# Layer 3 of a four-layer network summed before v is projected, its residual kept token-major, and the first layer's statistics on ScalarE

## The chip, the cores and the metric

The kernel runs on one core of one Trainium2 chip. The metric is the device time of the whole program in microseconds, the median of three runs. The engines are TensorE (PE, with PEld for its weight loads), VectorE (DVE), ScalarE (ACT), GpSimd (POOL) and SyncE (SP, which only issues transfers here).

## The reference

Sixteen images of 64 x 64 tokens with 256 channels in float32 go through four layers. Each layer adds to the residual what it makes of the group-normalised residual (32 groups):

```python
x = x + _L0_conv_ref(_gn(x), embeddings)      # nearest of 1024 code vectors, by distance
x = x + _L1_conv_ref(_gn(x), Wf, bf, ...)     # per row of 64 tokens: sigmoid(f g^T) h
x = x + _L2_conv_ref(_gn(x), w1, b1, ...)     # softmax over 4096 tokens of x0[i] x1[j]; a gate per token
x = x + _L3_conv_ref(_gn(x), w_qkv, w_out, b_out, gamma, beta)
...
def _L3_conv_ref(x, w_qkv, w_out, b_out, gamma, beta):      # 4 heads of 32
    q, k, v = jnp.split(jnp.einsum('bxyc,cf->bxyf', x, w_qkv), 3, axis=-1)
    q, k, v = (to_bhcn(q), to_bhcn(k), to_bhcn(v))
    q = jax.nn.softmax(q, axis=-2) * SCALE
    k = jax.nn.softmax(k, axis=-1)
    context = jnp.einsum('bhdn,bhen->bhde', k, v)
    out = jnp.einsum('bhde,bhdn->bhen', context, q)
    ...
    out = jnp.einsum('bxyh,hc->bxyc', out, w_out) + b_out
    mu = jnp.mean(out, axis=-1, keepdims=True)
    var = jnp.mean(jnp.square(out - mu), axis=-1, keepdims=True)
    return (out - mu) * jax.lax.rsqrt(var + LN_EPS) * gamma + beta
```

## The kernel before, in words

One image is one batch `b` of 4096 tokens, worked on in eight chunks of 512 tokens (four tiles of 128). The residual travels between layers through DRAM, channel-major: two blocks of 128 channels by 512 tokens, 512 KB a chunk. Each layer is a Python generator that emits its instructions and yields now and then. A heap of tasks with due times in units of a batch (`task`, the constants `LAG*` and `LEN*`) decides which generator emits next, so while one batch is in the search, the batches before it are in layer 1, in the exponentials of layer 2, in the gate and in layer 3. Blocks under `high_priority` are put ahead. A tile scheduler then lays the instructions into each engine's order and adds the waits; each engine works through its own order, and so does SP through its transfers.

The stages, with the lines of the profile:

- `stats0` (L298) takes the statistics of the input by DVE's `bn_stats` (L254). `gn_finish` turns statistics into scale and mean (L261 to L277).
- `stage1`, the search: `norm` (L327, L330) normalises on ACT; per tile of 128 tokens, PE makes the products with 1024 codes (`pd`, L382), ACT the norms (`nn`, L377), DVE finds the largest (L389, L394) and POOL gathers and adds the code to the tokens (L395). `back` transposes the chunk to channel-major (L357), ACT copies it out of PSUM (L360), DVE takes the next layer's statistics (L254, `st_s<-xt_s`), and ACT's queue stores it.
- `layer1`: projections (L465, L476), scores, tanh (L497), mixing (L509, L513).
- `rows2`, `stage2`: three rows of projections (L567), then 64 pairs a batch of an exponential over 2048 columns on ACT (`ex`, L619) and a product-and-sum on DVE (L622). `gate2` applies the gate (L675, L676) and takes statistics.
- `stage3`, layer 3, in two passes over the chunks. First pass: k (`pk`, L729) with a running maximum, exp (L738), q and v in one product of 256 columns a tile (`pqv`, L751), their bias as a row in three bfloat16 parts (`qv_row`, L755; `put_row` makes it), the transposed exp(k) (`ek`, L762, L764), q's softmax (maximum L770, subtraction on POOL L771, exp L772, sum L774, division on POOL L776), the context sum over k and v (`pc`, L780, L782), and one chunk later q transposed (L717, L719) and stored by ACT's queue. Between the passes the context goes through the output projection (`wctx`) and a Gram matrix (`gram`), from which the variance of an output row is q^T gram q. Second pass: `form` loads q and multiplies (`pz` L821, `qz` L823), `variance` sums by a product with ones (`pvr`, L829) and takes the power -1/2 on POOL (L832). The output is `po` (L849), scaled on ACT (L852), and the residual, read from DRAM again, is transposed with its row added (`pxo`, L854, L858) and added on DVE (L860).

The PSUM pool `ps_m` has four banks of 512 float32 columns, shared by all stages; `ps_w` has two of 1024.

Of the kernel before, what the change touches and what calls it, by code (L numbers as in the profile page):

```python
# [41 lines left out]
def kernel(  # L42
# [82 lines left out]
    def row_tile(name):  # L125
        t = const.tile([P, 2, C], BF16, name=name)
        nc.gpsimd.memset(t, 0.0)
        return t

    h_row, qv_row, x_row = row_tile("h_row"), row_tile("qv_row"), row_tile("x_row")  # L130

    def put_row(dst, v, weight, tag, plus=None):
# [4 lines left out]
        row = pb[:PARTS, :C]  # L137
        weight(row, v3, plus)

        for n in range(PARTS - 1):  # L140
            top = small.tile([PARTS, C], BF16, tag="ptop", name=f"top_{tag}_{n}", bufs=1)
            nc.scalar.copy(top, row)
            nc.tensor.matmul(row, lhsT=below[:, n, :], rhs=top, start=False, stop=True, skip_group_check=True)
        nc.scalar.copy(dst[0:PARTS, :, :], row.unsqueeze(1).to_broadcast([PARTS, 2, C]))
# [43 lines left out]
    w_src = w_qkv.rearrange("(k p) (s n) -> p k s n", p=P, s=3)  # L188


    gam = s3p.tile([P, C], F32, tag="v2", name="gam", bufs=5)
    nc.scalar.dma_start(out=gam, in_=gamma.rearrange("(o n) -> o n", o=1).to_broadcast([P, C]))

    def centred(src, name):
        t = const.tile([P, 2, C], F32, name=name)
        nc.scalar.dma_start(out=t[:, 0, :], in_=src)
        m = small.tile([P, 1], F32, tag="cen", name=f"cen_{name}")
        nc.vector.tensor_reduce(m, t[:, 0, :], AX.X, ALU.add)
        nc.vector.tensor_scalar(m, m, -1.0 / C, None, ALU.mult)
        nc.vector.tensor_scalar(t[:, 0, :], t[:, 0, :], m, None, ALU.add)  # L200
        nc.vector.tensor_tensor(t[:, 1, :], t[:, 0, :], gam, ALU.mult)
        return t

    wo2 = centred(w_out, "wo2")


    bo2 = centred(b_out.rearrange("(o n) -> o n", o=1).to_broadcast([P, C]), "bo2")
    nc.vector.tensor_scalar(bo2, bo2, float(DH ** 0.5 / HEADS), None, ALU.mult)

# [46 lines left out]
    def gn_finish(st, kind, b):  # L256

        tag = f"{kind}_{b}"
        mv = small.tile([P, NK, 2], F32, tag="gn_mv", name=f"mv_{tag}")
        for k in range(NK):  # L260
            nc.vector.bn_aggr(mv[:, k, :], st[:, k, :, :].rearrange("p c s -> p (c s)"))  # L261
        mean = mv[:, :, 0]
# [45 lines left out]
    def stage1(b):  # L308
        tag = f"s1_{b}"
        scale, _, nbias = norm0.pop(b)  # L310
# [39 lines left out]
        st1 = stats_tile(1, f"st1_{tag}")  # L350
        x1_d[b] = []

        def back(ch):
            for k in range(NK):
# [5 lines left out]
                nc.scalar.copy(xt[ch][:, k, :], pt)  # L360
            chunk_stats(st1, xt[ch], ch)
# [10 lines left out]
        for ch in range(NCHUNK):  # L372
            for t in range(CH):
# [27 lines left out]
                if t == 1:  # L401
                    if ch + 1 < NCHUNK:
                        norm(ch + 1)
                        yield 2
                if t == 2:
                    if ch + 1 < NCHUNK:
                        norm_rows(ch + 1)
                    if ch > 0:
                        back(ch - 1)
                        yield 2  # L410
                if t == 3:
                    if ch + 1 < NCHUNK:
# [4 lines left out]
        with tc.high_priority(offset=URGENT):  # L417
            norm1[b] = gn_finish(st1, "n1", b)
# [5 lines left out]
    def layer1(b):  # L424
# [34 lines left out]
        def attend(ch):  # L459
# [14 lines left out]
            for t in range(CH):  # L474
# [5 lines left out]
                if t % 2 == 1:  # L480
                    nc.tensor.matmul(
                        ph[:, t - 1 : t + 1, :], lhsT=ones3, rhs=h_row, start=False, stop=True, skip_group_check=True
# [207 lines left out]
    def stage3(b):  # L690
# [6 lines left out]
        wqv_n = wts.tile([P, NK, 2 * P], F32, tag="wqv_n", name=f"wqv_{tag}")  # L697
        nc.sync.dma_start(out=wqv_n[:, :, 0:P], in_=w_src[:, :, 0, :])
        nc.sync.dma_start(out=wqv_n[:, :, P:], in_=w_src[:, :, 2, :])
        with tc.high_priority(offset=URGENT):  # L700
            scaled(wk_n, scale, nc.scalar)
            scaled(wqv_n, scale, nc.vector)
            put_row(qv_row, nmean, by_weight(wqv_n), f"qv_{tag}")
# [6 lines left out]
        ctxa = wts.tile([P, P], F32, tag="ctxa", name=f"ctx_{tag}")  # L710
        qvs, qTs = {}, []
# [228 lines left out]
```

## Time and profile before

| | |
|---|---|
| median of three runs | 5996.47 us (5990.2 to 6000.28) |
| profiled execution: time, span | 5985.76 us, 5984.0 us |
| granted TensorE clock, mean | 0.949 |
| busy PE, DVE, ACT, POOL | 5310.6, 5132.9, 4756.8, 1873.7 us |
| DMA | 1059.10 MB, mean 177 GB/s |

A page of the profile lists each engine's busy time, the chain of work that ended last, and the costliest groups of instructions: line, engine, operation, output and inputs by the program's names, shape, count, busy time, mean duration of one in ns, then the idle time ahead of them and who ended it. A float32 product appears as two records on PE. A wait line gives the waiting engine and line, the one it waited for, the total in us, the number of times and the longest.

### The profile page before, as it was taken

What the parts mean: (1) busy time and instruction counts of PE and PEld (TensorE: products, weight loads), DVE (VectorE), ACT (ScalarE), POOL (GpSimd) and SP (SyncE); (2) the same over time, 40 slices, a digit from 0 to 9 for tenths busy, and PEclk for the clock granted to TensorE, in tenths of its full rate; (3) what the DMA queues carried; (4) which work ended last, traced back from release to release, by engine and by line L of the source; (5) the groups of instructions that cost most, each with busy time, mean ns of one, the idle gap of its engine ahead of it and who ended that gap; (6) DMA issues with size and microseconds to landing.
All of it is one profiled execution on the core that took longest, in us unless ns stands there. A gap on an engine that the chain in (4) does not pass through costs nothing.

```text
span 5984.0 us, 73947 instructions
## 1 busy us (share of the span) xinstructions
PE 5310.6 (89%) x25167; PEld 3208.0 (54%) x25167; DVE 5132.9 (86%) x7270; ACT 4756.8 (79%) x7138; POOL 1873.7 (31%) x1314
## 2 busy tenths in 40 slices
PE   8978798989989899998989989898999989887777
PEld 3535355545556465554646556464655646464445
DVE  6589698899989899898989989898998989888862
ACT  4578597878888797888979788797988879787763
POOL 3222224233332333323333332433333333312231
PEclk9989899999999999999999999999999999998788
DMA  6453645665656657565665746566475655545543
GB/s 185 143 160 112 209 132 186 187 187 158 207 165 201 194 160 227 149 210 163 197 212 156 224 151 207 172 199 203 153 223 160 204 183 172 188 140 176 170 144 111
DMA packets 521359, 1059.10 MB, mean 177 GB/s; under 512 B 52504, under 2 KB 266392, under 8 KB 512792
## 3 DMA queue, kind: packets, MB, share of 16 engines
q1 hardware_dynamic: 406288, 885.11, 44.6%
q0 software_dynamic: 73728, 67.14, 7.8%
q10 hardware_dynamic: 40968, 102.13, 4.5%
q8 instruction: 200, 3.28, 0.2%
q14 instruction: 175, 1.43, 0.1%
HBM read 751.18 MB, written 303.04 MB: 176 GB/s over the span
## 4 chain that ended last, share of the span: by engine, by line
PE 48%; DVE 21%; ACT 15%; issue 7%; DMA 5%; POOL 4%; ACTq 0%; SPq 0%; POOLq 0%; DVEq 0%
PE pd_s L382 16%; DVE ex_s L622 10%; ACT ex_s L619 6%; PE ph_l L476 4%; PE pqv_s L751 4%; PE po_s L849 3%; DVE i_s L394 2%; PE pk_s L729 2%; PE pr_r L567 2%; DVE nd_s L389 2%; PE po_l L509 2%; POOL xc_s L395 2%; PE pvr_s L829 1%; DVE st_s L254 1%; PE pc_s L780 1%
## 5 line engine op out<-in xcount | busy, mean ns | idle before, releaser
L622 DVE CUSTOM_DVE_ANT_0 ex_s<-ex_s,x2b 128x2048 f32<-128x2048 f32 x1024 | 2369.4, 2318 | 135.9 <-ACT ex_s L619 133.5
L619 ACT ACTIVATE ex_s<-x0b,nmax_s,x_r 128x2048 f32<-128x2048 f32 x1024 | 2138.8, 2089 | 64.7 <-DVE num_s L622 55.0
L382 PE MATMUL pd_s<-e,xn_s 128*128 128x512 f32 x4096 | 2013.5, 621 | 87.6 <-DVE m L389 63.8
L395 POOL DMA_INDIRECT xc_s<-in_emb_rows,i_s x512 | 1084.0, 2117 | 1962.9 <-DVE i_s L394 1460.6
L382 PEld LDWEIGHTS pd_s<-e,xn_s 128*128 128x128 f32 x4096 | 750.6, 196 | 830.4 <-issue 655.0
L389 DVE CUSTOM_DVE_ANT_0 nd_s<-pd_s,nn_s 128x1024 f32<-128x1024 f32 x512 | 620.5, 1212 | 114.8 <-PE pd_s L382 85.4
L394 DVE FIND_INDEX8 i_s<-m,nd_s 128x8 uint32<-128x1024 f32 x512 | 623.5, 1218 | 0.0
L377 ACT ACTIVATE nn_s<-ne,nx_s 128x1024 f32<-128x1024 f32 x512 | 585.1, 1145 | 10.6 <-DVE nx_s L348 3.4
L476 PE MATMUL ph_l<-wh_l,xt_l 128*128 128x256 f32 x2048 | 534.6, 396 | 28.6 <-DVE xt_l L513 20.6
L751 PE MATMUL pqv_s<-wqv_s,xk_s 128*128 128x256 f32 x2048 | 491.9, 381 | 2.9 <-ACT xt_s L360 2.9
L476 PEld LDWEIGHTS ph_l<-wh_l,xt_l 128*128 128x128 f32 x2048 | 381.7, 194 | 155.1 <-issue 61.2
L751 PEld LDWEIGHTS pqv_s<-wqv_s,xk_s 128*128 128x128 f32 x2048 | 388.4, 191 | 130.1 <-issue 63.3
L832 POOL TENSOR_TENSOR lrs_s<-lrs_s,mhalf 128x4 f32<-128x4 f32 x128 | 187.6, 1465 | 651.5 <-ACT lrs_s L831 638.0
L849 PE MATMUL po_s<-wctx_s,qo_s 128*128 128x256 f32 x1024 | 329.4, 412 | 63.5 <-ACT y_s L852 59.8
L852 ACT ACTIVATE y_s<-po_s,lrs_s 128x256 f32<-128x256 f32 x512 | 236.0, 470 | 147.5 <-PE po_s L849 104.3
L327 ACT ACTIVATE xn_s<-xt_s,nb_n,s_n 128x512 f32<-128x512 f32 x256 | 202.4, 806 | 108.2 <-DMA xt_s<-in_xT 98.6
L776 POOL TENSOR_TENSOR qv_s<-qv_s,qd_s 128x512 f32<-128x512 f32 x128 | 167.2, 1307 | 385.3 <-DVE qd_s L775 312.8
L509 PE MATMUL po_l<-attn,h_l 128*128 128x128 f32 x2048 | 280.7, 283 | 7.3 <-DVE m L389 5.2
L509 PEld LDWEIGHTS po_l<-attn,h_l 128*128 128x128 f32 x2048 | 259.9, 195 | 45.8 <-issue 22.1
L849 PEld LDWEIGHTS po_s<-wctx_s,qo_s 128*128 128x128 f32 x1024 | 178.0, 199 | 194.5 <-ACT y_s L852 123.9
L729 PE MATMUL pk_s<-xk_s,wk_s 128*128 128x512 f32 x512 | 256.6, 623 | 0.0
L860 DVE TENSOR_TENSOR y_s<-pxo_s,y_s 128x512 f32<-128x512 f32 x256 | 174.1, 683 | 91.4 <-ACT y_s L852 91.3
(197 smaller groups left out, 7707.6 us busy)
## 6 DMA issues: line engine op xcount, KB each, us to landing
xs_s<-in_xT SPq DMA_DIRECT2D x128, 512.0 KB
xt_s<-in_xT SPq DMA_DIRECT2D x128, 512.0 KB
xc_s<-in_x SPq DMA_DIRECT2D x128, 512.0 KB
x_s<-xt_s ACTq DMA_DIRECT2D x128, 512.0 KB
xt_l<-x_s SPq DMA_DIRECT2D x128, 512.0 KB
x_l<-xt_l SPq DMA_DIRECT2D x128, 512.0 KB
xr_r<-x_l SPq DMA_DIRECT2D x128, 512.0 KB
xg_g<-x_l SPq DMA_DIRECT2D x128, 512.0 KB
```

The source lines that it names most:

```text
L377: nc.scalar.activation(nn, ne2, AF.Identity, bias=nx2[ch][:, t : t + 1])
L382: nc.tensor.matmul(pd[:, cols], lhsT=xn[ch][:, k, t * P : (t + 1) * P], rhs=e2[:, k, cols], start=(k == 0), stop=(k == NK - 1),)
L389: nc.vector.tensor_tensor_reduce(out=nd, in0=pd, in1=nn, scale=1.0, scalar=-3.0e38, op0=ALU.add, op1=ALU.max, accum_out=m8[:, 0:1],)
L394: nc.vector.max_index(i8, m8, nd)
L395: nc.gpsimd.indirect_dma_start(out=xc[ch][:, t, :], out_offset=None, in_=emb_rows, in_offset=bass.IndirectOffsetOnAxis(ap=i8[:, 0:1], axis=0),
L476: nc.tensor.matmul(ph[:, t, :], lhsT=X[:, k, t * P : (t + 1) * P], rhs=wh_n[:, k, :], start=(t % 2 == 0 and k == 0), stop=False, skip_grou ...
L509: nc.tensor.matmul(po[:, k, t * P : (t + 1) * P], lhsT=hs[ch][:, t, k * P : (k + 1) * P], rhs=at[:, t, :], start=True, stop=True,)
L619: nc.scalar.activation(ex, x0b, AF.Exp, bias=nmax[:, T : T + 1], scale=x01[:, T, 1:2], accum_out=den[:, h, T : T + 1])
L622: nc.vector.tensor_tensor_reduce(out=ex, in0=ex, in1=x2b, scale=1.0, scalar=0.0, op0=ALU.mult, op1=ALU.add, accum_out=num[:, h, T : T + 1],)
L729: nc.tensor.matmul(pk, lhsT=wk_n[:, k, :], rhs=xt[:, k, :], start=(k == 0), stop=(k == NK - 1))
L751: nc.tensor.matmul(pqv[:, j, :], lhsT=xt[:, k, t * P : (t + 1) * P], rhs=wqv_n[:, k, :], start=(j == 0 and k == 0), stop=False, skip_group ...
L849: nc.tensor.matmul(po[:, j, :], lhsT=qT[:, t * P : (t + 1) * P], rhs=wctx[:, 1, :], start=True, stop=True)
```

## The change

Layer 3 no longer projects v for every token. The residual is transposed to token-major (with its row added) in the first pass; the products with exp(k) sum it over the tokens, 256 columns wide (`gather`), and the sum of a batch is projected by v's weights afterwards, between the passes. q is projected alone; `gather` and the division of q's softmax (`normalize`) follow one chunk later. The token-major residual is stored by ACT's queue and read again in the second pass, where DVE scales the output and adds the residual in one instruction. q is stored token-major by SP and transposed in the second pass; the variance is the sum of a product taken by DVE, tile by tile. Loads of q run two chunks ahead, those of the residual one. The bias rows are kept once and read repeated. In the search, `back` takes the statistics by accumulators of two ACT passes (a copy, and a Square written back to PSUM), and it now comes before `norm`. `gn_ends` is the second half of `gn_finish`. The first batch's layer 1 is given 0.2 of a batch in place of 0.35.

```diff
-    h_row, qv_row, x_row = row_tile("h_row"), row_tile("qv_row"), row_tile("x_row")
+    h_row, q_row, x_row = row_tile("h_row", C), row_tile("q_row", P), row_tile("x_row", C)
+
+    def repeated(row, n):
+        return row.unsqueeze(1).to_broadcast([P, n, row.shape[-1]])
...
-        st1 = stats_tile(1, f"st1_{tag}")
+
+        st1 = small.tile([P, 2, NK, NCHUNK], F32, tag="gn_st1", name=f"st1_{tag}", bufs=1)
...
-                nc.scalar.copy(xt[ch][:, k, :], pt)
-            chunk_stats(st1, xt[ch], ch)
+                nc.scalar.activation(xt[ch][:, k, :], pt, AF.Copy, accum_out=st1[:, 0, k, ch : ch + 1])
+                nc.scalar.activation(
+                    pt, pt, AF.Square, bias=nshift[:, k : k + 1], accum_out=st1[:, 1, k, ch : ch + 1]
+                )
...
-                if t == 1:
-                    if ch + 1 < NCHUNK:
-                        norm(ch + 1)
-                        yield 2
-                if t == 2:
+                if t == 1 and ch > 0:
+                    back(ch - 1)
+                    yield 2
+                if t == 2 and ch + 1 < NCHUNK:
+                    norm(ch + 1)
+                    yield 2
+                if t == 3:
...
-            norm1[b] = gn_finish(st1, "n1", b)
+            mv = small.tile([P, NK, 2], F32, tag="gn_mv", name=f"mv_{tag}")
+            sums = small.tile([P, 2, NK], F32, tag="gn_sum", name=f"sum_{tag}", bufs=1)
+            off = small.tile([P, NK], F32, tag="gn_off", name=f"off_{tag}", bufs=1)
+            nc.vector.tensor_reduce(sums, st1, AX.X, ALU.add)
+            nc.vector.tensor_scalar(mv[:, :, 0], sums[:, 0, :], 1.0 / TOK, None, ALU.mult)
+            nc.vector.tensor_tensor(off, mv[:, :, 0], nshift, ALU.add)
+            nc.vector.tensor_tensor(off, off, off, ALU.mult)
+            nc.vector.scalar_tensor_tensor(
+                mv[:, :, 1], sums[:, 1, :], 1.0 / TOK, off, op0=ALU.mult, op1=ALU.subtract
+            )
+            norm1[b] = gn_ends(mv, "n1", b)
...
+        def normalize(ch):
+            qd = small.tile([P, CH, HEADS], F32, tag="qd", name=f"qd_{tag}_{ch}")
+            nc.vector.tensor_reduce(qd, heads(ch), AX.X, ALU.add)
+            nc.vector.reciprocal(qd, qd)
+            nc.gpsimd.tensor_tensor(heads(ch), heads(ch), qd.unsqueeze(3).to_broadcast([P, CH, HEADS, DH]), ALU.mult)
+
+        def gather(ch):
+            pc = bank(f"pc_{tag}_{ch}")
+            ek, xr = eks.pop(ch), res.pop(ch)
             for t in range(CH):
+                nc.tensor.matmul(pc[:, :C], lhsT=ek[:, t, :], rhs=xr[:, t, :], start=(t == 0), stop=(t == CH - 1))
+            if ch > 0:
+                nc.vector.scalar_tensor_tensor(
+                    sums, sums, al[:, ch : ch + 1], pc[:, :C], op0=ALU.mult, op1=ALU.add
+                )
+            else:
+                nc.vector.tensor_copy(sums, pc[:, :C])
+
+        def store_q(ch):
+            d = dram.tile([P, CH, P], F32, tag=f"q_{ch}", name=f"qd_{tag}_{ch}")
+            nc.sync.dma_start(out=d, in_=q4s.pop(ch))
+            qds.append(d)
...
         for ch in range(NCHUNK):
             xt = xb.tile([P, NK, CW], F32, tag="xb", name=f"xk_{tag}_{ch}")
             nc.sync.dma_start(out=xt, in_=x3[ch])
+            if ch > 0:
+                normalize(ch - 1)
...
-            qv = s3p.tile([P, CH, 2, P], F32, tag="u4", name=f"qv_{tag}_{ch}")
...
+            q4s[ch] = s3p.tile([P, CH, P], F32, tag="q4", name=f"q_{tag}_{ch}", bufs=3)
+            pq = bank(f"pq_{tag}_{ch}").rearrange("p (t d) -> p t d", d=P)
+            for t in range(CH):
+                for k in range(NK):
+                    nc.tensor.matmul(
+                        pq[:, t, :], lhsT=xt[:, k, t * P : (t + 1) * P], rhs=wq_n[:, k, :],
+                        start=(t == 0 and k == 0), stop=False, skip_group_check=True,
+                    )
+            nc.tensor.matmul(pq, lhsT=ones3, rhs=repeated(q_row, CH), start=False, stop=True, skip_group_check=True)
+            nc.scalar.copy(q4s[ch], pq)
             if ch == 0:
                 put_row(x_row, xm_, by_identity, f"x_{tag}")
-            yield 5
+            if ch > 0:
+                gather(ch - 1)
+            yield 4
+
+            qm = small.tile([P, CH, HEADS], F32, tag="qm", name=f"qm_{tag}_{ch}")
+            nc.vector.tensor_reduce(qm, heads(ch), AX.X, ALU.max)
...
-                nc.tensor.matmul(pc[:, :P], lhsT=ek[:, t, :], rhs=qv[:, t, 1, :], start=(t == 0), stop=(t == CH - 1))
...
-        def form(ch):
-            qs[ch] = s3p.tile([P, CW], F32, tag="qo", name=f"qo_{tag}_{ch}")
...
+            xr = s3p.tile([P, CH, C], F32, tag="xr", name=f"xt_{tag}_{ch}", bufs=3)
+            res[ch] = xr
+            for pr in range(CH // 2):
                 px = bank(f"pxo_{tag}_{ch}_{pr}").rearrange("p (j c) -> p j c", c=C)
                 for j in range(2):
                     t = 2 * pr + j
                     for k in range(NK):
                         nc.tensor.matmul(
                             px[:, j, k * P : (k + 1) * P], lhsT=xt[:, k, t * P : (t + 1) * P], rhs=ident,
                             is_transpose=True, start=(j == 0 and k == 0), stop=False, skip_group_check=True,
                         )
+                nc.tensor.matmul(px, lhsT=ones3, rhs=repeated(x_row, 2), start=False, stop=True, skip_group_check=True)
+                nc.scalar.copy(xr[:, 2 * pr : 2 * pr + 2, :], px)
+            d = dram.tile([P, CH, C], F32, tag=f"xr_{ch}", name=f"xd_{tag}_{ch}")
+            nc.scalar.dma_start(out=d, in_=xr)
+            xds.append(d)
+            nc.scalar.activation(q4s[ch], q4s[ch], AF.Exp)
+            if ch > 0:
+                store_q(ch - 1)
+            yield 6
+        gather(NCHUNK - 1)
+        normalize(NCHUNK - 1)
...
+            nc.scalar.activation(sums, sums, AF.Copy, scale=rk)
+            pt = bank(f"pct_{tag}")
+            for k in range(NK):
+                nc.tensor.transpose(pt[:, k * P : (k + 1) * P], sums[:, k * P : (k + 1) * P], ident)
+            sumT = wts.tile([P, NK, P], F32, tag="wT", name=f"sT_{tag}")
+            for k in range(NK):
+                nc.scalar.activation(
+                    sumT[:, k, :], pt[:, k * P : (k + 1) * P], AF.Identity, bias=vm[:, k : k + 1]
+                )
+
+            pw = bank(f"pcx_{tag}")
+            for k in range(NK):
+                nc.tensor.matmul(
+                    pw[:, :P], lhsT=wv_n[:, k, :], rhs=sumT[:, k, :], start=(k == 0), stop=(k == NK - 1)
+                )
...
+        def load(ch):
+            qs[ch] = s3p.tile([P, CH, P], F32, tag="q4", name=f"qo_{tag}_{ch}", bufs=3)
+            nc.sync.dma_start(out=qs[ch], in_=qds[ch])
+
+        def queries(ch):
+            pq = bank(f"pqt_{tag}_{ch}")
+            for t in range(CH):
+                nc.tensor.transpose(pq[:, t * P : (t + 1) * P], qs[ch][:, t, :], ident)
+            qTs[ch] = s3p.tile([P, CW], F32, tag="v2", name=f"qT_{tag}_{ch}", bufs=3)
+            nc.scalar.activation(qTs[ch], pq, AF.Copy, scale=float(DH ** -0.5))
+
+        def variance(ch):
+            q = qs.pop(ch)
+            pz = bank(f"pz_{tag}_{ch}")
+            for t in range(CH):
+                nc.tensor.matmul(
+                    pz[:, t * P : (t + 1) * P], lhsT=qTs[ch][:, t * P : (t + 1) * P], rhs=gram, start=True, stop=True
+                )
+            rss[ch] = small.tile([P, CH], F32, tag="ln_rs", name=f"lrs_{tag}_{ch}")
+            for t in range(CH):
+                nc.vector.tensor_tensor_reduce(
+                    out=q[:, t, :], in0=pz[:, t * P : (t + 1) * P], in1=q[:, t, :], scale=1.0, scalar=0.0,
+                    op0=ALU.mult, op1=ALU.add, accum_out=rss[ch][:, t : t + 1],
+                )
+            nc.scalar.activation(rss[ch], rss[ch], AF.Identity, bias=eps3)
+            nc.gpsimd.tensor_tensor(rss[ch], rss[ch], mhalf, ALU.pow)
+
+        def residual(ch):
+            xrs[ch] = s3p.tile([P, CH, C], F32, tag="xr", name=f"xo_{tag}_{ch}", bufs=3)
+            nc.sync.dma_start(out=xrs[ch], in_=xds[ch])
+
+        load(0)
+        queries(0)
+        yield 2
+        load(1)
+        variance(0)
+        residual(0)
+        yield 3
+        before = None
+        for ch in range(NCHUNK):
+            qT, rs, xr = qTs.pop(ch), rss.pop(ch), xrs.pop(ch)
+            for pr in range(2):
                 if pr == 0 and before is not None:
                     nc.sync.dma_start(out=dst[:, (ch - 1) * CH : ch * CH, :], in_=before)
+                po = bank(f"po_{tag}_{ch}_{pr}").rearrange("p (j c) -> p j c", c=C)
+                for j in range(2):
+                    t = 2 * pr + j
+                    nc.tensor.matmul(
+                        po[:, j, :], lhsT=qT[:, t * P : (t + 1) * P], rhs=wctx[:, 1, :], start=True, stop=True
+                    )
+                    nc.vector.scalar_tensor_tensor(
+                        xr[:, t, :], po[:, j, :], rs[:, t : t + 1], xr[:, t, :], op0=ALU.mult, op1=ALU.add
+                    )
                 if ch + 1 < NCHUNK:
-                    (form, variance)[pr](ch + 1)
+                    if pr == 0:
+                        residual(ch + 1)
+                        queries(ch + 1)
+                    else:
+                        if ch + 2 < NCHUNK:
+                            load(ch + 2)
+                        variance(ch + 1)
                 yield 3
-            before = y
+            before = xr
...
-        end = task("layer1", b + 1 + LAG1, LEN1 if left and b else 0.35, layer1(b), 88)
+        end = task("layer1", b + 1 + LAG1, (LEN1 if b else 0.2) if left else 0.35, layer1(b), 88)
```

## The prediction

> **What bounds the kernel now.** I read the page's busy shares first, then the chain that ended last, then the costly groups, then the windows, then who waits for whom, then the end of the run.
>
> ```profile
> PE 5310.6 (89%) x25167; PEld 3208.0 (54%) x25167; DVE 5132.9 (86%) x7270; ACT 4756.8 (79%) x7138; POOL 1873.7 (31%) x1314
> PE 48%; DVE 21%; ACT 15%; issue 7%; DMA 5%; POOL 4%; ACTq 0%; SPq 0%; POOLq 0%; DVEq 0%
> PE pd_s L382 16%; DVE ex_s L622 10%; ACT ex_s L619 6%; PE ph_l L476 4%; PE pqv_s L751 4%; PE po_s L849 3%; DVE i_s L394 2%; PE pk_s L729 2%; PE pr_r L567 2%; DVE nd_s L389 2%; PE po_l L509 2%; POOL xc_s L395 2%; PE pvr_s L829 1%; DVE st_s L254 1%; PE pc_s L780 1%
> ```
>
> No engine is alone: PE 89%, DVE 86%, ACT 79%. The chain spends 48% on PE and 21% on DVE. The window from 1000 to 5200 us, where all stages of twelve batches run side by side, is closer still:
>
> ```profile
> 1000.00:5200.00 4200.00, 3854.69 (x18614) 2337.34 (x18613) 3793.28 (x5333) 3522.16 (x5277) 1392.27 (x947) 0.97 0.60 186
> ```
>
> That is PE 92%, DVE 90%, ACT 84%, POOL 33%, clock 0.97, DMA 60%: 350 us a batch, in which PE leaves 29 us free and DVE 34. PE's figure flatters: eight pd_s records of 621 ns take 3.70 us in the timeline, 0.43 us from start to start, so 4096 of them need 1.76 ms of the 2013.5 us they show. DVE's records overlap by under 0.1 us, so its 90% is real. The rows that the change touches:
>
> ```profile
> L751 PE MATMUL pqv_s<-wqv_s,xk_s 128*128 128x256 f32 x2048 | 491.9, 381 | 2.9 <-ACT xt_s L360 2.9
> L852 ACT ACTIVATE y_s<-po_s,lrs_s 128x256 f32<-128x256 f32 x512 | 236.0, 470 | 147.5 <-PE po_s L849 104.3
> L860 DVE TENSOR_TENSOR y_s<-pxo_s,y_s 128x512 f32<-128x512 f32 x256 | 174.1, 683 | 91.4 <-ACT y_s L852 91.3
> ```
>
> DVE's own waits, by the table of waits, total 851 us; the ones that layer 3 and the search own are these:
>
> ```profile
> DVE y_s L860 <- ACT y_s L852: 91.3, 60, 5.6
> DVE qd_s L774 <- ACT qv_s L772: 70.6, 57, 3.0
> DVE st_s L254 <- ACT xt_s L360: 54.6, 32, 4.1
> DVE ctx_s L782 <- PE pc_s L780: 52.5, 45, 3.4
> DVE qz_s L823 <- PE pz_s L821: 42.6, 29, 3.9
> ```
>
> The reader should see that each is a consumer placed right behind its producer. At the end of the run (5500 to 5984 us) the chain has one more member, a transfer waited for by name, 9.9% of 484 us or 48 us:
>
> ```profile
> by line: DVE ex_s L622 13.8%; DMA qo_s<-qd_s 9.9%; PE po_s L849 7.4%; PE pqv_s L751 7.2%; PE pz_s L821 7.0%; issue 4.5%; PE pk_s L729 4.5%; ACT ex_s L619 3.6%; PE pvr_s L829 3.2%; PE pxo_s L854 2.6%; PE pc_s L780 2.4%; POOL qv_s L771 2.3%;
> ```
>
> **What the Trainium skill says.** "Perfetto Trace Analysis", section Identifying the Most-Contended Engine: matmul busy time is not a good measure, for pipelined matmuls overlap in the records. The 621 ns against 0.43 us above agree, so I do not count PE's removed busy time in full. "ScalarE: Activation LUTs", section What ACT_TABLE_LOAD costs: a per-partition bias or scale operand adds about 93 ns; here kx (with one) takes 675 ns and qT (without) 601, so 74. "Perfetto Trace Analysis", section Matmuls: matmul groups should rotate through PSUM banks so that draining one overlaps filling the next; the pool `ps_m` has four, and PE's waits on the drains (pd_s on DVE 63.8 us, po_s on ACT 59.8) show that this is not always enough. "TensorE: Matmul & The Clock Gate", Part 1: idle windows of PE lower its clock. The trace agrees: 0.97 where PE is 92% busy, 0.74 in the 60 us from 5600 where it is 61%.
>
> **The change, part by part** (layer 3 runs 16 x 8 = 128 chunks, and an f32 product is two records).
>
> PE. Out: pqv 491.9 us and its bias rows 96.9 (L755); pc at 128 columns 159.4; pvr 133.1 (L829); pz as 256 records of 512 columns 147.3. In: q alone, 2048 records of 128 columns at the rate of po_l (280.7 us for 2048, L509), 281; one bias row a chunk, 48; pc at 256 columns at pqv's 0.240 us a record, 1024 of them, 246; pz as 1024 records of 128 columns, 141. The transposes of q and of the residual stay in number and only move. 716 in, 1029 out: **PE -313 us**. The bias rows are now read repeated from one copy; no row shows that, so 0, at worst twice the 0.21 us start to start of a bf16 row for 640 of them, +134 busy.
>
> DVE. Out: the first layer's statistics on the chunk (L254, st_s<-xt_s) 163.8, y 174.1, qz 87.2: 425. In: 512 reduces of 128 columns out of PSUM. L389 (1024 columns, 1212 ns) and L622 (2048, 2318) give 1.08 ns a column over 106 ns, so 244 ns and 82 for the read of the accumulator: 167 us; L795's 286 ns would make it 188. And 512 scale-and-add of 256 columns out of PSUM: between L782 (128: 341) and L800 (512: 745) that is 476 ns, 244 us; bounds 424 (a plain 256-column add, L201) to 520, 217 to 266. The update of the sums grows from 341 to 476 ns, +15; small statistics +3. **DVE +4**, bounds -25 to +50.
>
> ACT. Out: y 236.0; one of the two q copies a chunk, 73. In: the residual's copies, 256 x 576 = 147; in `back` the copy becomes an activation with an accumulator (601 + 196, as qT and kx's read, for 584: +55) and a Square with one follows (675 + 196: +223). **ACT +116 us**. No table switch: the trace has one ACT_TABLE_LOAD in all, with Exp and Square already mixed.
>
> POOL keeps its passes. DMA: x3 is read once instead of twice, the residual is written and read: +67 MB on 1059, share 0.60 to about 0.64. ACT's queue issues as many transfers, SP's one more a chunk, 128 x 0.32 = 41 us of SP. Behind SP's wait for the store of chunk ch-2 (the residual's three buffers) stand the search's loads; ACT already waits 98.6 us for those (xn on xt_s), so I bound this at 0 to +50 and take 5.
>
> What lies on the path. pqv holds 4% of the chain, 239 us for 492 us busy, so half of it is exposed. By that half: q for qv (211 us less busy) -102; the bias rows (-48) -24; pc (+87) +43; pz 0. pvr, 1% of the chain or 60 us, goes whole: -60. DVE is on the chain for 0.245 of its busy time and ACT for 0.19: +1 and +22. Sum: **-120 us**.
>
> Waits. y, qd, st_s go (216 us); ctx and qm find their data ready, some 50 more. In their place DVE must now wait for po (ACT waited 104.3 us for it, and 36.1 for POOL's lrs) and for pz as before. The net, 266 less 140 or 126 us, is DVE idle time; at DVE's 0.245, -31, which I cut to -10 since ACT is fuller. What is late next is ACT's exp for L622, 133.5 us already.
>
> End. Now q is asked for two chunks ahead and the residual one: of the 48 us of qo transfers -30 should go. Last phase: 59 us for eight chunks (5925 to 5984), of 1.28 MB each; at the 262 GB/s of the best 60 us early on, 39. Against it the longer tail of products between the phases (scale, two more transposes, two copies, two products), +4 once; elsewhere other batches cover it. Net -25. First batch's layer 1 from 0.35 to 0.2 of a batch: it only pulls layer 1 forward while exps of batch 1 are bound to their own layer 1; 0, bounds -15 to +15. `back` before `norm` in the search: norm keeps one tile of about 11 us for 3.2 us of ACT work; 0, bounds 0 to +30.
>
> Sum: -120 + 5 - 10 - 25 = **-150 us** on the profiled execution's 5985.76 (span 5984.0), which stands 10.7 below the median of 5996.47. On the median: **5846 us**, -2.5%.
>
> **Rivals.** (1) PE is the whole bound: then all 313 us return and the end's 25, 5996 - 338 = 5658, damped by its clock to about 5690. For it: 48% of the chain. Against: 0.43 us against 621 ns, and DVE would stand at 95%. (2) DVE is the bound and its work does not shrink: only its waits do. With 90% and a little less waiting it gives 20 to 70 us, 5926 to 5976. For it: its 90% is real; PE's gain then becomes PE idle time. (3) Slower, by PSUM banks: `back`'s two banks are held for about 1.67 us by ACT instead of 0.58, pz for 1.3 by DVE instead of 0.68, po by DVE, which runs 2.3 us instructions between. That is 256 + 128 + 256 = 640 holdings on four banks; PE in order stops behind a full one, with the search's pd_s queued behind it. At 0.25 us each it eats 160 us and the gain is gone; at 0.4 us, 256 us, it gives 5846 + 256 = 6102. Against: the banks per chunk fall from twelve to ten. (4) The residual's round trip holds SP and returns the gain: 5990; DMA at 60% speaks against it.
>
> **Numbers.** My forecast, 5780 to 5910: 0.50. Rival 1: 0.14. Rival 2: 0.22, nearly all of it beyond 0.2% (12 us), which is about what a measurement of this kernel can tell from no change. Rival 3: 0.10. Rival 4: 0.04. Rival 2 gives 0.20 of it to faster and 0.02 to the same, rival 4 all to the same: faster 0.84, same 0.06, slower 0.10. The range takes in most of rival 1's way and nearly all of rival 2: 5710 to 5970.
>
> **What would show it.** Right: PE near 5000 us, DVE within 50 of 5133, ACT near 4870; the scale-and-add at 476 ns and the reduce at 244; no wait of DVE on y, on qd or on st_s; the transfer of q off the chain at the end; a batch of about 342 us in the middle window (350 less a sixteenth of 125). Wrong: a batch still above 347 us with PE's idle time grown by 240 us or more (rival 2); new waits of PE on drains of pt, pz, po beyond 150 us (rival 3); SP's waits for the residual followed by ACT's xn on its load (rival 4).

## The result, and the profile after

The change makes the kernel slower: 6141.48 us, median of four runs (6125.07 to 6161.39), against 5998.38 for the kernel before in the same call; ratio 1.0241, 95% interval 1.0208 to 1.0274. The profiled execution spans 6139.1 us at a mean granted clock of 0.920, against 5984.0 us at 0.949. First the busy line of the page after, then the answer for the window from 1000 to 5200 us (its length, then busy PE, PEld, DVE, ACT, POOL with instruction counts, clock, DMA share, GB/s):

```profile
PE 5216.7 (85%) x24863; PEld 3172.1 (52%) x24863; DVE 5113.4 (83%) x8228; ACT 4815.5 (78%) x7570; POOL 1957.3 (32%) x1330
```

```profile
1000.00:5200.00 4200.00, 3667.93 (x17636) 2232.54 (x17635) 3640.38 (x5802) 3447.84 (x5408) 1423.77 (x924) 0.93 0.61 191
```

PE has 94 us less to do and DVE 20 less, yet the span grew by 155: idle time grew on all three, PE's from 673 to 922 us. In the window PE, DVE and ACT are each busy for less of the same 4200 us than before, and the clock fell from 0.97 to 0.93. The rows of the new work, from the groups of after, and what now waits, from its table of waits:

```profile
L920 DVE SCALAR_TENSOR_TENSOR xo_s<-po_s,lrs_s,xo_s 128x256 f32<-128x256 f32 x512 | 239.5, 479 | 127.0 <-POOL lrs_s L895 70.4 <-PE po_s L917 54.4 <-issue 1.0
L890 DVE CUSTOM_DVE_ANT_0 qo_s<-pz_s,qo_s 128x128 f32<-128x128 f32 x512 | 121.0, 286 | 17.8 <-PE pz_s L885 17.6
L890 DVE DVE_READ_ACCUMULATOR2_ANT lrs_s<- 128x1 f32 x512 | 43.3, 85 | 0.0
L366 ACT ACTIVATE pt_s<-pt_s,nm_n 128x512 f32<-128x512 f32 x256 | 167.6, 655 | 0.0
L366 ACT ACTIVATION_READ_ACCUMULATOR pt_s<-pt_s,nm_n 128x1 f32 x256 | 52.3, 204 | 0.0
```

```profile
ACT ex_s L633 <- DVE num_s L636: 187.8, 150, 4.2
...
DVE qd_s L739 <- ACT q_s L823: 68.6, 46, 6.0
PE pt_s L362 <- DMA xc_s<-in_emb_rows,i_s: 68.6, 24, 7.6
...
PE po_s L917 <- DVE xo_s L920: 65.1, 65, 3.4
```

The costs of the rows came close to what was worked out. The waits did not: ACT's exponentials wait 187.8 us for DVE, and PE's transposes in `back` wait for POOL's gather 24 times. The same two waits before:

```profile
ACT ex_s L619 <- DVE num_s L622: 55.0, 49, 4.7
...
PE pt_s L357 <- DMA xc_s<-in_emb_rows,i_s: 35.3, 9, 6.6
```

Where the time is lost shows when the profiled run is cut at the search of each batch, which begins with its first FIND_INDEX8 on `i_s`: the time up to the seventh batch's search, the nine batches from there to the sixteenth's search, and the rest.

| | before | after |
|---|---|---|
| seventh search starts | 1719 us | 1788 us |
| per batch, seventh to sixteenth | 353.1 us | 365.0 us |
| of it idle on PE, DVE, ACT | 28.0, 34.7, 56.9 | 44.2, 47.2, 65.2 |
| from the sixteenth search to the end | 1087.4 us | 1066.5 us |

The end is 21 us shorter; the loss is in the stages that run side by side, 12 us a batch and 69 on the way there.

### The profile page after: what moved, and what is told of

Read it like the earlier page. It is cut to its first block, busy times and chain, and to the rows that moved or that the text cites. A ratio compares the mean times of both kernels' runs of the same rounds, so it can differ in the third digit from the quotient of the medians.

```text
span 6139.1 us, 74780 instructions
## 1 busy us (share of the span) xinstructions
PE 5216.7 (85%) x24863; PEld 3172.1 (52%) x24863; DVE 5113.4 (83%) x8228; ACT 4815.5 (78%) x7570; POOL 1957.3 (32%) x1330
## 5 line engine op out<-in xcount | busy, mean ns | idle before, releaser
L633 ACT ACTIVATE ex_s<-x0b,nmax_s,x_r 128x2048 f32<-128x2048 f32 x1024 | 2138.7, 2089 | 194.2 <-DVE num_s L636 187.8
L490 PEld LDWEIGHTS ph_l<-wh_l,xt_l 128*128 128x128 f32 x2048 | 393.0, 198 | 166.6 <-DVE xt_l L527 56.9
L917 PE MATMUL po_s<-wctx_s,qT_s 128*128 128x256 f32 x1024 | 337.0, 427 | 68.4 <-DVE xo_s L920 65.1
L523 PE MATMUL po_l<-attn,h_l 128*128 128x128 f32 x2048 | 307.6, 301 | 64.0 <-DVE xt_l L527 55.4
L895 POOL TENSOR_TENSOR lrs_s<-lrs_s,mhalf 128x4 f32<-128x4 f32 x128 | 241.3, 1885 | 336.4 <-ACT lrs_s L894 327.0
L920 DVE SCALAR_TENSOR_TENSOR xo_s<-po_s,lrs_s,xo_s 128x256 f32<-128x256 f32 x512 | 239.5, 479 | 127.0 <-POOL lrs_s L895 70.4
L786 PEld LDWEIGHTS pq_s<-wqv_s,xk_s 128*128 128x128 f32 x2048 | 257.1, 196 | 89.5 <-issue 61.4
L917 PEld LDWEIGHTS po_s<-wctx_s,qT_s 128*128 128x128 f32 x1024 | 182.7, 207 | 190.1 <-DVE xo_s L920 116.3
L786 PE MATMUL pq_s<-wqv_s,xk_s 128*128 128x128 f32 x2048 | 258.5, 279 | 12.5 <-ACT attn L511 12.5
L747 PE MATMUL pc_s<-xt_s,ek_s 128*128 128x256 f32 x1024 | 266.3, 402 | 0.9 <-ACT xt_s L819 0.9
L741 POOL TENSOR_TENSOR q_s<-q_s,qd_s 128x512 f32<-128x512 f32 x128 | 160.9, 1257 | 326.5 <-DVE qd_s L740 255.5
L800 POOL TENSOR_TENSOR q_s<-q_s,qm_s 128x512 f32<-128x512 f32 x128 | 181.0, 1414 | 238.7 <-DVE qm_s L799 75.4
```

The lines of the kernel that those rows point to most:

```text
L490: nc.tensor.matmul(ph[:, t, :], lhsT=X[:, k, t * P : (t + 1) * P], rhs=wh_n[:, k, :], start=(t % 2 == 0 and k == 0), stop=False, skip_grou ...
L523: nc.tensor.matmul(po[:, k, t * P : (t + 1) * P], lhsT=hs[ch][:, t, k * P : (k + 1) * P], rhs=at[:, t, :], start=True, stop=True,)
L633: nc.scalar.activation(ex, x0b, AF.Exp, bias=nmax[:, T : T + 1], scale=x01[:, T, 1:2], accum_out=den[:, h, T : T + 1])
L786: nc.tensor.matmul(pq[:, t, :], lhsT=xt[:, k, t * P : (t + 1) * P], rhs=wq_n[:, k, :], start=(t == 0 and k == 0), stop=False, skip_group_c ...
L917: nc.tensor.matmul(po[:, j, :], lhsT=qT[:, t * P : (t + 1) * P], rhs=wctx[:, 1, :], start=True, stop=True)
```

## The experiments

Two parts first: layer 3 alone (e1), the search alone (e2), and of the search the order alone (e4); e3 is meant to take away SP's wait for q. e1 is the change with the search and the length of layer 1 as before (the excerpt shows lines taken out and put back), e2 the kernel before with the search alone as in the change:

```diff
-                nc.scalar.activation(xt[ch][:, k, :], pt, AF.Copy, accum_out=st1[:, 0, k, ch : ch + 1])
...
+                nc.scalar.copy(xt[ch][:, k, :], pt)
+            chunk_stats(st1, xt[ch], ch)
...
-                if t == 1 and ch > 0:
-                    back(ch - 1)
...
+                if t == 1:
+                    if ch + 1 < NCHUNK:
+                        norm(ch + 1)
...
-        end = task("layer1", b + 1 + LAG1, (LEN1 if b else 0.2) if left else 0.35, layer1(b), 88)
```

> Layer 3 of the changed kernel alone: the search keeps bn_stats on DVE, its old order (norm, then back) and the first batch's layer 1 its old length. Theory search (the loss lies in the search: statistics on ACT and norm one tile later): 5830 to 5900 us, a batch under 350 us. Theory SP (the store of q waits on SP for POOL's division and the search's loads queue behind it): 6080 to 6160. Theory drain (DVE waits for POOL's power and drains PSUM late): 6080 to 6160.

e1 ran at 6107.68 us, ratio 1.0178 (1.0159 to 1.0197): layer 3 alone loses 112 us.

> The kernel before with the search's part alone: statistics on ACT and back ahead of norm; layer 3 and lengths as before. Theory search: 6100 to 6250 us. Theories SP and drain: 5960 to 6040, DVE 164 us less busy and ACT 275 us more.

e2 ran at 6072.28 us, 1.0124 (1.0108 to 1.0141): the search alone loses 76, although DVE's busy time fell by 143 us, to 4990.

e3, the change with

```diff
-            if ch > 0:
-                store_q(ch - 1)
             yield 6
...
+            if ch > 1:
+                store_q(ch - 2)
             if ch > 0:
                 normalize(ch - 1)
             pk = bank(f"pk_{tag}_{ch}")
...
```

> The changed kernel with the store of q put half a chunk later in SP's program, behind the next chunk's load, so that POOL's division is done when SP comes to it. Theory SP: 5850 to 6020 us, and DVE's wait for the loads of the statistics (81 us) falls under 30. Theories search and drain: 6110 to 6170.

e3 ran at 6134.97 us, 1.0228 (1.0211 to 1.0245), like the change itself. But the wait that it was to remove is still there. First SP's wait for q in the change, then in e3:

```profile
SPq L757 <- POOL q_s L741: 625.4, 109, 18.8
```

```profile
SPq L757 <- POOL q_s L741: 612.3, 107, 19.7
```

In the order of SP's transfers one of the 128 stores of q alone stands elsewhere than in the change, so e3 says nothing on what this wait costs. What speaks against it as the cause of layer 3's loss is that it is nearly as long in e8 below (493 us) as in e1 (504), although these two kernels lie 114 us apart.

e4, the kernel before with `back` at t == 1 and `norm` at t == 2, as in the change:

> The kernel before with only the order in the search turned: back at a chunk's second tile, norm at its third; statistics stay on DVE. Theory search, if the order is its cause: 6080 to 6200 us, with DVE waiting over 50 us for ACT's nn (14 before). If ACT's longer back is its cause, or theories SP and drain: 5980 to 6020.

e4 ran at 6026.28 us, 1.0044 (1.0027 to 1.0061): the order costs 30 us here. Its table of waits has PE's wait for the gather 24 times again, in place of 9, and DVE's wait for ACT's norms `nn`, which the expectation named. The second fence has the latter in the kernel before:

```profile
DVE nd_s L389 <- ACT nn_s L377: 68.7, 50, 2.5
...
PE pt_s L357 <- DMA xc_s<-in_emb_rows,i_s: 55.2, 24, 7.7
```

```profile
DVE nd_s L389 <- ACT nn_s L377: 14.2, 18, 3.2
```

`back` transposes the tokens that POOL's gather has just added the codes to. One tile earlier, the last gather of the chunk more often has not landed, and PE, which works in order, stops. The edit also makes `norm` later, and with it `nn`, for which DVE now waits 54 us more. No run moved one of the two alone.

e5, statistics alone, is the kernel before with `back` of the change in its old place.

> The kernel before with only the first layer's statistics moved to ACT's accumulators; the order of back and norm stays as before. Both search edits together cost 76 us and the order alone 30. If the two add up, this runs at about 6042 us (+46) with ACT's busy time 174 us up and DVE's 143 us down, so DVE gives back nothing for what it is relieved of. If the order was what hurt and only shows in full with the longer ACT work, it runs within 15 us of before. If relief of DVE is worth what its share of the chain says, it runs at about 5960 us. Rival (PSUM banks held by ACT): PE's waits on drains by ACT in the search grow by 40 us or more.

e5 ran at 6052.85 us, 1.0085 (1.0054 to 1.0116): the moved statistics lose 53 us by themselves.

Next, layer 3's two new jobs of DVE are undone in e1, one by one and together. e6 gives the scaling of the output back to ACT:

```diff
-                    nc.vector.scalar_tensor_tensor(
-                        xr[:, t, :], po[:, j, :], rs[:, t : t + 1], xr[:, t, :], op0=ALU.mult, op1=ALU.add
-                    )
+                    nc.scalar.activation(po[:, j, :], po[:, j, :], AF.Copy, scale=rs[:, t : t + 1])
+                two = xr[:, 2 * pr : 2 * pr + 2, :]
+                nc.vector.tensor_tensor(two, po, two, ALU.add)
```

> Layer 3's change alone (6108 us), but the output's product po is again scaled by ACT, in place in PSUM, 256 columns at a time, and DVE adds two tiles at once (512 columns), as before the change. Theory (PE and DVE wait for each other at the output, and ACT's exponentials for DVE): DVE's busy time falls by about 65 us and ACT's rises by about 236; DVE's waits for po (10 us a batch more than before) and PE's waits for the adding go; the time falls by 60 us or more to about 6040. Rival (the rest of layer 3's new shape, its reduces or its first pass, costs the time): it stays within 20 us of 6108, or gets slower since ACT is fuller.

e6 ran at 6033.57 us, 1.0046 (1.0024 to 1.0067), 74 less than e1. e7 gives the sum of the variance back to PE:

```diff
+            nc.tensor.matmul(pz, lhsT=gram, rhs=qTs[ch], start=True, stop=True)
+            prod = q.rearrange("p t d -> p (t d)")
+            nc.vector.tensor_tensor(prod, pz, qTs[ch], ALU.mult)
+            pv = bank(f"pvr_{tag}_{ch}")
             for t in range(CH):
-                nc.vector.tensor_tensor_reduce(
...
+                nc.tensor.matmul(pv[:, t : t + 1], lhsT=prod[:, t * P : (t + 1) * P], rhs=one, start=True, stop=True)
...
```

> Layer 3's change alone (6108 us), but the variance as before: one product of 512 columns, one DVE multiplication of 512 columns from PSUM, and a sum by products with ones. DVE's busy time falls by about 110 us (121 for the reduces with their accumulators' reads against 87, and fewer instructions), PE's rises by about 130. Theory DVE load (the period of a batch follows DVE's busy time, at 90% of it): the time falls by 80 us or more. Theory of the output's drain: it stays within 25 us, for po is drained as in the change.

e7 ran at 6087.40 us, 1.0146 (1.0114 to 1.0177), 20 less than e1. The expectation's 110 us off DVE was wrong: its busy time fell by 30, since the reduces kept it busy for 123 us and the multiplication that comes back takes 87.

> Layer 3's change alone (6108 us) with both of these undone: output scaled by ACT, variance summed by PE. If DVE's load in layer 3 is the whole cause, this runs at or under the kernel before (5996), for q alone, pc and the bias rows still save PE some 180 us. If the cause is the first pass (residual transposed there, gather and division a chunk later), it stays above 6060.

e8, both, ran at 5993.37 us, 0.9989 (0.9980 to 0.9998): all of layer 3's loss is back. Is it that DVE is in the way at the output, or DVE's load as such? e9 gives e8 a useless instruction that nothing waits for but the store:

```diff
                 nc.vector.tensor_tensor(two, po, two, ALU.add)
+                nc.vector.tensor_scalar(two, two, 1.0, None, ALU.mult)
```

> The kernel of e8 (layer 3's change with output scaled by ACT and variance by PE, 5993 us) with a useless DVE instruction after each addition at the output: the 512 columns just added, in SBUF, times 1 (256 instructions, an estimate of 0.33 us each from the 512-column rows out of SBUF, 85 us in all: as much DVE busy time as e8 took from e1). It waits for nothing new, holds no PSUM bank and only the store follows it. Theory DVE load (any work of DVE lengthens the batch): the time rises by 85 to 115 us to about 6080 to 6110, as in e1. Theory drain (it counts only where DVE stands between PE's product, its bank and ACT's exponential): it rises by under 45 us.

e9 ran at 6133.25 us, 1.0218 (1.0201 to 1.0235): 140 us more for 87 of DVE's busy time. The busy line of the page of e1:

```profile
PE 5191.6 (85%) x24863; PEld 3159.5 (52%) x24863; DVE 5262.7 (86%) x8436; ACT 4633.4 (76%) x6802; POOL 1846.7 (30%) x1330
```

That of e8, and then the row of the distance product `pd_s` from e8's groups:

```profile
PE 5188.4 (87%) x25119; PEld 3146.7 (53%) x25119; DVE 5178.4 (87%) x7284; ACT 4803.8 (80%) x7314; POOL 1883.9 (32%) x1330
```

```profile
L387 PE MATMUL pd_s<-e,xn_s 128*128 128x512 f32 x4096 | 2014.6, 625 | 161.6 <-DVE m L394 82.3 <-DVE xt_l L518 54.7 <-ACT xn_s L331 19.6
```

The same two of e9:

```profile
PE 5268.7 (86%) x25119; PEld 3181.8 (52%) x25119; DVE 5265.8 (86%) x7540; ACT 4812.4 (78%) x7314; POOL 1867.1 (30%) x1330
```

```profile
L387 PE MATMUL pd_s<-e,xn_s 128*128 128x512 f32 x4096 | 2044.6, 634 | 173.7 <-DVE m L394 93.2 <-DVE xt_l L518 52.8 <-ACT xn_s L331 19.6
```

DVE's busy time over the median time is 0.862, 0.863, 0.860, 0.864, 0.859 in e1, e6, e7, e8, e9: among these five, time goes up and down with DVE's work. That the time grew by more than the 87 us goes with a lower clock: e8 and e9 have the same 25119 records on PE, `pd_s` takes 634 ns in place of 625, and PE's busy time grew by 80 us while the mean granted clock fell from 0.939 to 0.925. One other way is open. The store that waits for the useless instruction stands in SP's order among the search's loads, and ACT's wait for these loads grew too. First e8, then e9:

```profile
ACT xn_s L331 <- DMA xt_s<-in_xT: 80.6, 25, 9.1
```

```profile
ACT xn_s L331 <- DMA xt_s<-in_xT: 114.8, 28, 7.3
```

How much of the 140 us came that way was not tried. The wait on the output itself is not what tells e1 from e8: PE with its weight loads waits 244 us for po's drain by DVE in e1 and 252 for the drain by ACT in e8.

e10 looks for the 21 us at the end: before, with q asked for one step earlier.

```diff
...
                     (form, variance)[pr](ch + 1)
+                if pr == 1 and ch + 2 < NCHUNK:
+                    load(ch + 2)
                 yield 3
```

> The kernel before, where the second pass of layer 3 asks for a chunk of q one step earlier than it uses it. In the change the end of the run after the last search got 17 to 23 us shorter; if that is the early load of q, this runs 15 to 25 us under before (5975). Rival (the shorter end comes from the residual, which is no longer transposed in the second pass): within 8 us of before.

e10 ran at 6001.53 us, 1.0008 (0.9996 to 1.0019). In its profiled run the last stretch is 1073 us, 14 shorter than before's, but what comes ahead of it gives that back (seventh search at 1726 us, 354.1 us a batch).

e11 is the change with the edits of e6 and e7.

> The change as it is (6141 us), with the output again scaled by ACT and the variance again summed by PE; the search's edits stay. If layer 3 and the search add up, it loses the 115 us that e8 gained over e1 and runs at about 6026. If ACT, now with the statistics of the search as well, is then the fullest engine, it gains under 60 us and stays above 6080.

e11 ran at 6157.63 us, 1.0252 (1.0225 to 1.0279): no gain, though DVE is 79 us less busy than in the change. With the search's edits in, DVE's work in layer 3 is not what the time follows. One suspect in the search is the PSUM bank that `back` keeps for the Square. e12 is e5 with

```diff
-                nc.scalar.activation(
-                    pt, pt, AF.Square, bias=nshift[:, k : k + 1], accum_out=st1[:, 1, k, ch : ch + 1]
-                )
+            for k in range(NK):
+                nc.scalar.activation(
+                    xc[ch][:, 2 * k : 2 * k + 2, :].rearrange("p t c -> p (t c)"), xt[ch][:, k, :], AF.Square,
+                    bias=nshift[:, k : k + 1], accum_out=st1[:, 1, k, ch : ch + 1]
+                )
```

> The kernel of e5 (before, with the first layer's statistics on ACT, 6053 us), but the Square reads the copy in SBUF and writes over the tokens already transposed, so a PSUM bank in back is held for the copy alone, as before the change; ACT's busy time stays within 25 us of e5's. Theory PSUM banks: the time falls by 35 us or more, to before's. Theory ACT load (the exponentials come later since ACT has 170 us more to do): it stays within 15 us of e5.

e12 ran at 6013.69 us, 1.0025 (1.0016 to 1.0034), 39 less than e5 at the same ACT load. The busy lines of e5 and e12:

```profile
PE 5321.9 (88%) x24872; PEld 3229.6 (53%) x25167; DVE 5012.1 (83%) x7062; ACT 4948.9 (82%) x7906; POOL 1805.0 (30%) x1314
```

```profile
PE 5325.0 (89%) x25167; PEld 3223.8 (54%) x25167; DVE 4998.6 (83%) x7062; ACT 4955.9 (82%) x7906; POOL 1814.7 (30%) x1314
```

The loads are alike, so reading SBUF in the Square is worth 39 us, 0.15 us for each of 256. The edit frees the bank after the copy, and it also lets the second copy go ahead of the first Square. That the bank is the reason is not shown: summed over the trace, PE waits 5 us for ACT's work in `back` and its weight loads 26 in e5, 0.3 and 31 in e12. What stays is telling: 134 us off DVE and 199 onto ACT make the kernel 18 us slower than before, not faster.

The same steps taken on the whole change, one after another: e13 has the Square from SBUF, e14 also the old order, e15 also the old length, e16 also the variance of e7.

> The change (6141 us) with the Square reading the copy in SBUF and writing over transposed tokens. Theory PSUM banks: it saves the 39 us that e12 saved over e5, or more, since layer 3 now also holds banks for DVE (pz, po): 6100 or less. Rival (the banks cost only where PE is as full as before the change): within 15 us of 6141.

> As e13, and norm comes before back in the search, as before the change. e4 puts the order at 26 to 30 us: this runs some 30 us under e13, at about 6070. Rival (order costs only because the Square stood behind it): within 10 us of e13.

> As e14, and the first batch's layer 1 has 0.35 of a batch again. The change reaches the seventh batch's search 69 us later than before (1788 against 1719) and the kernels with the old length at 1723 to 1760. If the length is behind that, this runs 15 to 40 us under e14; if the order was, within 10 us of it. In all this is layer 3's change alone (6108, DVE 5263 us) with 143 us of DVE's statistics on ACT without a held bank: theory DVE load gives about 6108 - 143 x 1.2 + e12's 18 = 5955, theory of three near-equal engines about 6040.

> As e15, and the variance summed by PE as before the change (DVE 30 us less, PE some 37 us more busy, as e7 showed). Theory DVE load: 20 to 40 us under e15. If DVE is no longer the fullest once it has lost the statistics: within 10 us of e15 or above it.

e13 ran at 6096.78 us (1.0147, 1.0120 to 1.0173), e14 at 6030.28 (1.0047, 1.0027 to 1.0068), e15 at 6029.32 (1.0049, 1.0035 to 1.0062), e16 at 6035.79 (1.0053, 1.0037 to 1.0070). The Square from SBUF is worth 45 us, the old order 67 (by the ratios 56 and 60), the length nothing, the variance nothing. PE's wait for the gather in e13 and in e14, from their tables of waits:

```profile
PE pt_s L362 <- DMA xc_s<-in_emb_rows,i_s: 67.3, 25, 7.5
```

```profile
PE pt_s L362 <- DMA xc_s<-in_emb_rows,i_s: 29.7, 9, 4.9
```

DVE's wait for `nn` fell by 6 us only, from 62.4 to 56.4, so here the gather is the likelier part of the order's cost.

e15 can also be read against e1: it is e1 with the first layer's statistics on ACT, the Square from SBUF. There 164 us off DVE and 193 onto ACT made the kernel 78 us faster, while the same move made the kernel before 18 us slower (e12).

The last two try to beat both kernels. e17 is e8 with the scaled output written to SBUF, so that po's bank does not wait for DVE's addition; e18 also gives ACT half of the first layer's statistics, from SBUF.

```diff
...
-                    nc.scalar.activation(po[:, j, :], po[:, j, :], AF.Copy, scale=rs[:, t : t + 1])
+                    nc.scalar.activation(y[:, j, :], po[:, j, :], AF.Copy, scale=rs[:, t : t + 1])
...
-                nc.vector.tensor_tensor(two, po, two, ALU.add)
+                nc.vector.tensor_tensor(two, y, two, ALU.add)
```

> The kernel of e8 (5993 us), but ACT writes the scaled output to SBUF, into the chunk of q that is no longer needed, and DVE adds from there: po's bank is held for ACT's two scalings alone and no longer until DVE has added. Engine work stays the same, except DVE's addition, which no longer reads PSUM. Theory PSUM banks: PE's waits on po's drain (78 us on PE, 173 on its weight loads) fall by a half and the time by 15 to 40 us, to 5955 to 5980, under the kernel before. Rival (these waits are not what the time follows): within 10 us of 5993.

> As e17, and of the first layer's statistics the second block of 128 channels is taken by ACT (copy with an accumulator, Square from SBUF), the first stays on DVE; norm before back. DVE loses some 72 us, ACT gains some 90. Theory DVE load: 20 to 60 us under e17. Theory three near-equal engines (work moved from DVE to ACT buys nothing): within 15 us of e17.

Both missed: e17 ran at 6022.47 us (1.0043, 1.0030 to 1.0056), e18 at 6047.62 (1.0085, 1.0059 to 1.0112). PE's waits on po's drain grew from e8 to e17 (PE 78 to 123 us, weight loads 173 to 219) although DVE's addition no longer holds the bank. The chunk of q that takes the output is now held longer, and its next load with it; whether that is the reason was not tried.

## Why the prediction was wrong, point by point

**The rows were right, within 45 us.** The scale-and-add takes 479 ns (forecast 476). A reduce takes 286 ns, but the 85 ns of its accumulator's read lie within that and the next reduce starts when that read does, so that all of them keep DVE busy for 122 us (forecast 167). PE's removed and added rows come to 1029 and 730 us (forecast 716 added). ACT's records sum to 117 us more (116), though its busy time, in which overlapping records count once, grew by 59 only. DMA traffic grew by 67 MB. The end is shorter by 21 us (25); asking for q earlier, the larger part of that forecast, shortened it by 14 in e10 and made the kernel no faster. The 5 us for SP stay untested, since e3 left SP's order nearly as it was.

**The step that failed is "What lies on the path", with its -120 us.** It priced PE's removed rows by their share of the chain, about half, and DVE's time at 0.245. PE's relief was not paid at that price: in e8, where PE is 122 us less busy than before and DVE and ACT some 46 more each, it bought 0.1%. No run relieved PE alone, so what it is worth by itself stays open. The relief was also smaller: PE's busy time fell by 94 us rather than 313: its untouched rows take some 200 us more, of which a clock of 0.920 for 0.949 accounts for about 135, an estimate from 3.15% of the 4282 us in those rows before.

DVE's +4 (measured: -20) was a net of two amounts that do not have the same price. Layer 3's part alone adds 130 us of DVE's busy time and 112 us of time, although PE is relieved at once (e1). Undoing 84 us of DVE's part returns 114 (e8), and 87 us of filler cost 140 (e9): 1.4 to 1.6 us of time for each us of DVE, some six times 0.245 (the variance's part alone, 20 for 30 in e7, is less). Taking the statistics off DVE returned nothing in the kernel before (e12, 134 us) and 78 us for 164 in layer 3's kernel (e15 against e1). Once they are off, less DVE work in layer 3 buys nothing (e11, 79 us; e16, 28 us). So the price of DVE's time hangs on the rest of the kernel.

What the limit is where it is nothing was not isolated: ACT, with 4956 us in e12 and 4987 in e11, and PE, in e12 89% busy as before, are the candidates, and no kernel here loaded one of them alone. In the change the statistics are off DVE, and undoing layer 3's load on DVE returned nothing there (e11): that load explains the loss of e1, not the 143 us of the change, which are taken apart under "The sum".

**"Waits": the list was of the wrong ones.** y and st_s went, but qd stayed at 68.6 us: the exponential now ends a chunk and the sum begins the next, so they are as close as before. The one that grew, ACT's exponential behind DVE's last sum, 55.0 to 187.8 us, was not priced. It is 269.3 us in e1 and 57.2 in e8, but 80.3 in e9, where DVE is as busy as in e1, so DVE's load alone does not set it.

**"`back` before `norm`: 0, bounds 0 to +30."** It costs 30 us on the kernel before and 67 in the change. The step looked at norm's slack and not at what `back` itself waits for, the gather one tile before. It also had norm's slack too large, if DVE's longer wait for `nn` (14.2 to 68.7 us in e4) is a part of the cost.

**The Square.** The Trainium skill, "Perfetto Trace Analysis", section Matmuls, wants the groups of PE to rotate through banks so that a drain is hidden. The Square kept `back`'s bank for longer, and reading SBUF instead returned 39 us alone and 45 in the change; that the gain came through the bank, no wait in the traces shows.

**The rivals.** Rival 3 had the sign and perhaps a part of the cause: what goes with `back`'s banks costs 0.15 to 0.18 us a holding rather than 0.4. Its other 384 holdings do not show: with pz held briefly again, e16 gains nothing, and e17, which frees po's bank earlier, is slower. Nor does its sign, new waits of PE on drains beyond 150 us: for po, PE and its weight loads wait 181 us against 184 before, and for the Square 62. Rival 2's sign did come (365 us a batch, 249 us more idle time on PE), and its premise was right in e1, but it foresaw a gain, since it took DVE's work as unchanged. Rival 1, PE as the whole bound, falls with e8, which keeps most of PE's saving and is hardly faster than before. Rival 4 was not tested, for e3 hardly changed SP's order; its sign is absent from the change, where ACT waits 19.0 us for the search's load against 98.6 before, but not from e1, with 122.7.

**The sum.** The Square 45 and the order 67 make some 111 of the 143 us. With both undone, e14 and e15 still stand 28 to 35 us above the kernel before, with some 35 us less DVE time, 150 less on PE and 70 more on ACT. This remainder stays open. No version here beats the kernel before by what can be told apart: e8, at 0.9989, is within 0.2% of it.

## What to carry to other kernels

When three engines are each some 80 to 90% busy, a change that is neutral in sum on an engine need not be neutral in time: test the added work and the removed work apart, for here the price of a us of DVE went from nothing to over 1. After a run, look whether the wait that the edit was to remove is gone; in e3 it was not. Before an instruction group is moved earlier in the order, look up what its first operand waits for, above all a transfer. Where a second pass over a PSUM tile is added and a copy in SBUF exists, try reading the copy; here that was worth 39 and 45 us.

## What was not expected of the hardware

More work on one engine can lengthen the records of another. With the same products, 87 us more of DVE work came with a clock of 0.925 in place of 0.939 and with 80 us more busy time on PE (e9 against e8). An estimate from these figures, 5188 us x 0.939 / 0.925, gives 79 us more, so the clock accounts for nearly all of it. Busy PE time that a change seems to add or fail to remove can thus be clock and not work. How much of the kernel's 140 us the slower clock makes up was not tried.
